# Which queue asks for the raw expert weights, and how a planner dates its loads, in a one-core decoder kernel

## The chip, the core and the metric

The kernel runs on one core of a Trainium2 chip. Its time is the device time of one execution in microseconds (us), the median of several runs. The engines are named as the profile names them: PE multiplies matrices, DVE works on vectors, ACT evaluates functions, POOL is a second, slower vector engine, and SP only issues transfers. POOL issues transfers too. Each engine works through its own instructions in order.

## What is computed

One decoder block in float32 on x of shape (16, 256, 256), with a layer norm after each of its three parts:

```python
x = _layernorm(x + attn(x))          # linear attention by cumulative sums, 32 heads
x = _layernorm(x + xattn(x, ctx))    # autocorrelation attention over the context
x = _layernorm(x + ffn(x))           # 8 experts in two branches, all of them weighted by a router
```

In the first part, a projection z = x @ in_proj_w is convolved over time. Its score columns give weights p = exp(...), its value columns give sines and cosines, and cumulative sums of these products over time are normalized, gated and projected back. The second part correlates queries and keys by Fourier transforms, keeps the best lags, and mixes the rolled values. In the third part, chains of weight matrices (W_Q with V_fwd, W_Q with W_inv and W_inv_exp, and so on) can be multiplied ahead of the data.

## The kernel before

**Stages.** The 16 sequences are worked on as 8 pairs. Each pair p goes through front (projection, convolution, scores; line 602), body (sines, cosines, cumulative sums, gating; 669), context (Fourier transform of the context and its keys and values; 896), back (924), attention (1056), router (1076) and experts (1152). Apart from the pairs, fold_weights (816) multiplies the weight chains once: it loads 18 tiles called raw (function raw, line 819; 256 KB each, but for one of 128 KB), multiplies them on PE into banks called w_ps, and ACT copies the products to the constants w_v, w_h, w_c and u_o, which router and experts read.

**Tile names.** In front, xc holds the transposed x, sc_ps and sc the scores (weights w_sc), in_ps and zc the projection (weights in_proj_w) and its convolution, ph the spread scores and g their product with a polynomial. In body, sn and ge are zc and g spread over partitions by transfers that SP issues (spread, line 665): zc must be ready, then sn is sent, then ACT takes sines of it, then DVE multiplies and sums. In context, ct is loaded, transformed through dft_ps, and multiplied in kv_ps. pv (line 516) holds small columns that front needs, and w_ri (521) is a small weight of body.

**Memory.** The raw tiles, the xc and ct tiles, and most tiles of context, router and experts share 19 slots of one size (SLABS, line 49; slab, line 493). A table of shares (line 461) lets raw tiles hold at most 11 of them at a time.

**The order.** No instruction is issued where it is written. Each call of an engine is noted (note, line 187), and at the end a planner (Work, line 114) decides the order and issues them all (give, line 445). Forward (273) simulates the engines with a cost for each instruction and always starts, on each engine, the ready instruction of lowest rank. The first rank is the place of the instruction's stage in the table PLACES (line 39). Backward (424) then gives each instruction a latest time from what comes after it: its readers, and the next instruction of its own engine. The latest times are the ranks of the next of 3 passes, and the shortest plan is kept.

**Loads.** A transfer that reads only inputs is marked as a fetch (line 208). From the second pass on, a fetch is not started before its latest time less 40 us (AHEAD, lines 122 and 276):

```python
ready = {o: max(0.0, late[o] - self.AHEAD) if late and o.fetch else 0.0 for o in self.ops}
```

Line 430 dates a fetch like every other instruction, so its latest time is also bounded by whatever follows it in the order of its issuing engine:

```python
t = min(end - o.lat, free[o.eng] - o.dur + self.LEAD[o.eng])
late[o], free[o.eng] = t, t
```

SP issues xc, in_proj_w, ct and all the transfers from tile to tile in front, body and experts. POOL issues every other load: pv, w_sc, the small constants, Wq, out_proj_w, the raw tiles, x, and the results.

Of the kernel before, what the change touches and what calls it, by code (L numbers as in the profile page):

```python
# [21 lines left out]
P = 128  # L22
# [14 lines left out]


PLACES = {
    "front": (0.95, 1.25, 4.3, 4.1, 4.0, 6.3, 4.8, 6.35, 8.75),  # L40
    "body": (0.35, -1.65, 1.6, 3.25, 1.95, 5.25, 3.85, 7.05, 8.6),
    "ctx": (0.85, 2.48, 1.4, 1.55, 1.9, 4.7, 0.3, 2.05, 2.55),
    "back": (3.4, -8.35, -6.05, -8.95, -7.9, -4.75, -7.45, -5.0, 0.8),
    "att": (0.1, -2.35, -3.95, -2.7, -6.8, 1.0, -0.0, 0.7, 3.5),
    "router": (0.35, 0.35, -2.05, 3.45, 4.3, 6.0, 5.65, 6.85, 5.55),
    "expert": (1.18, 3.85, 3.95, 5.85, 5.8, 8.6, 5.95, 9.15, 13.2),
    "fold": (6.5, 1.66),
}
EARLY, SLABS, XT_BUFS, ZC_BUFS, KBUFS, VBUFS, X_BUFS = 3, 19, 1, 4, 2, 3, 9
AHEAD = range(1, NP)  # L50
# [63 lines left out]
class Work:  # L114
# [72 lines left out]
    def note(self, eng, op, issue, args, kw):  # L187
        aps = [v for v in list(args) + list(kw.values()) if isinstance(v, bass.AP)]
        out = kw.get("out", aps[0])
        ins = [v for v in aps if v is not out]  # L190
        o = self.last
        if not (eng == "PE" and o and o.eng == "PE" and (self.joins or o.tiles[-1] == out.tensor.name)):
            o = Op(len(self.ops), eng, self.rank)
            self.ops.append(o)
        self.last = o
        o.parts.append((issue, args, kw))
        d, lat, o.lock = self.cost(eng, op, out, ins)
        if eng == "PE":
            r, c = ins[0].ap[0][1], self.columns(ins[0])
            r0, c0 = ins[0].offset // math.prod(ins[0].tensor.shape[1:]), out.offset // math.prod(out.tensor.shape[1:])  # L200
            cells = [(i, j) for i in range(r0 // 32, (r0 + r + 31) // 32) for j in range(c0 // 32, (c0 + c + 31) // 32)]
            o.mm.append((d, cells))
            o.shape = r, c
        else:
            o.dur, o.lat = d, lat
        if op == "dma_start":
            o.size = 4 * self.columns(out) * out.ap[0][1]
            o.fetch = not any(hasattr(i.tensor, "tag") for i in ins)
        if op == "activation":
            o.table = self.SETS.get(args[2])  # L210
        for ap in ins + [out]:
            t = ap.tensor
            if not hasattr(t, "tag"):
                continue
            write = ap is out
            p0, p1, f0, f1 = self.box(ap)
            self.tiles.setdefault(t.name, (t, []))[1].append(o)
            keep = []
            for a in self.users.get(t.name, ()):
                q, w, a0, a1, b0, b1 = a  # L220
                meets = q is not o and a0 < p1 and p0 < a1 and b0 < f1 and f0 < b1
                if meets and (w or write):
                    o.pre[q] = o.pre.get(q, False) or w
                if not (write and meets and p0 <= a0 and a1 <= p1 and f0 <= b0 and b1 <= f1):
                    keep.append(a)
            keep.append((o, write, p0, p1, f0, f1))
            self.users[t.name] = keep

            if t.name in o.tiles:
                o.tiles.remove(t.name)  # L230
            o.tiles.append(t.name)
# [192 lines left out]
    def backward(self, starts, span):  # L424

        free = dict.fromkeys(self.LEAD, span)
        late = {}
        for o in sorted(self.ops, key=lambda o: (-starts[o][1], -o.k)):
            end = min([span] + [late.get(q, span) - self.gap(o, q, q.pre[o]) for q in o.then])
            t = min(end - o.lat, free[o.eng] - o.dur + self.LEAD[o.eng])  # L430
            late[o], free[o.eng] = t, t
        return late

    def run(self, passes):
# [21 lines left out]
def decoder_kernel(ctx: ExitStack, tc: tile.TileContext, a: dict, out: bass.AP):  # L456
# [5 lines left out]
    V, S, G, T, Y = (  # L462
        Later(work, name, eng)
        for name, eng in (
            ("DVE", nc.vector), ("ACT", nc.scalar), ("POOL", nc.gpsimd), ("PE", nc.tensor), ("SP", nc.sync)
        )
    )
# [10 lines left out]
    def chunked(name):  # L478
        v = a[name]
        if len(v.shape) == 3:  # L480
            return v.rearrange("(c p) g n -> p c g n", p=P)
        return v.rearrange("(c p) n -> p c n", p=P)

    def load(name, shape, chunks=False, pool=const, eng=Y, tag=None):
        t = pool.tile(shape, F32, name=name, tag=tag or name)
        eng.dma_start(out=t, in_=chunked(name) if chunks else a[name])
        return t
# [5 lines left out]
    def slab(shape, name):  # L493
        return new(ff, shape, "slab", SLABS, name)
# [4 lines left out]
    def f_bank(name):  # L499
        return new(f_ps, [P, 512], "fps", 4, name)  # L500
# [13 lines left out]
    ident = const.tile([P, P], F32, name="ident", tag="ident")  # L514
    make_identity(nc, ident)
    pv = load("pv", [P, NPV], eng=G)
    w_in = load("in_proj_w", [P, 2, 2 * D], True)
    w_sc = load("w_sc", [P, 2, 2, 32], True, eng=G)
    tcol = load("theta_col", [P, 8], eng=G)
    ones_bd = load("ones_bd", [P, 8, 32], eng=G)  # L520
    w_ri = load("w_ri", [P, 2, K], eng=G)
# [294 lines left out]
    def fold_weights():  # L816
        work.rank = work.place("fold", 0, 0.0)

        def raw(name, n):

            if n <= D:
                t = slab([P, 2, n], "raw")
                G.dma_start(out=t, in_=chunked(name))
                return t[:, 0, :], t[:, 1, :]
            both = [slab([P, n], "raw") for _ in range(2)]
            for c in range(2):
                G.dma_start(out=both[c], in_=chunked(name)[:, c, :])
            return both

        def eights(ap, br):  # L830
            return ap.rearrange("p (n s e) -> p n s e", s=2, e=8)[:, :, br, :]

        def product(left, right, n, dst):

            for blk in range(2):
                ps = f_bank("w_ps")
                for c in range(2):
                    T.matmul(
                        ps[:, :n], left[c][:, blk * P : (blk + 1) * P], right[c], start=c == 0, stop=c == 1
                    )  # L840
                to = dst(blk)
                S.copy(to, ps[:, :n] if len(to.shape) == 2 else ps.rearrange("p (n e) -> p n e", e=8))

        wq_ = raw("W_Q", D)
        product(wq_, raw("V_fwd", KR), KR, lambda blk: eights(w_v[:, blk, :], 0))
        r1 = raw("r1t", D)
        product(wq_, r1, D, lambda blk: w_h[:, blk, 0, :])
        wk_ = raw("W_K", D)
        product(wk_, raw("W_fwd", KR), KR, lambda blk: eights(w_c[:, blk, :], 0))

        w_inv = raw("w_inv_t", D)

        def inverse_of(weight):
            t = slab([P, 2, D], "inv")
            product(w_inv, weight, D, lambda blk: t[:, blk, :])
            return t[:, 0, :], t[:, 1, :]

        iq = inverse_of(wq_)
        product(iq, raw("W_inv_exp", KR), KR, lambda blk: eights(w_v[:, blk, :], 1))
        product(iq, r1, D, lambda blk: w_h[:, blk, 1, :])  # L860
        product(inverse_of(wk_), raw("V_inv", KR), KR, lambda blk: eights(w_c[:, blk, :], 1))
        wo_, bt = raw("wot", D), raw("bt", P)
        for i, name in enumerate(("U_0", "U_1")):
            u = raw(name, KR)
            for half in range(2):
                lo = half * 2 * P
                product(
                    [t[:, lo : lo + 2 * P] for t in u], wo_, D, lambda blk: u_o[:, i * 4 + half * 2 + blk, :]
                )
        ps = f_bank("w_ps")  # L870
        for c in range(2):
            T.matmul(ps[:, :D], bt[c], wo_[c], start=c == 0, stop=c == 1)
        V.tensor_copy(b_o, ps[:, :D])
# [477 lines left out]
```

## Time and profile before

| | |
|---|---|
| median of 3 runs | 856.03 us (855.74 to 857.06) |
| the profiled execution | 857.1 us, its span in the profile 855.3 us |
| mean granted PE clock | 0.989 of full speed |
| busy PE / DVE / ACT / POOL | 812.4 / 700.0 / 581.8 / 256.9 us |
| chain of waits, largest shares | PE 65%, DVE 13%, ACT 8%, DMA 7% |
| transfers | 103.30 MB, mean 121 GB/s |
| first and last w_ps matmul | 24.4 and 72.1 us |

The slices cut the span into 40 equal parts, with one digit each: busy share in tenths. In the timeline a line gives the start in us, the duration in us, the engine, the line of the code, the instruction, what it writes and reads, and the count; the bracket at the end holds the idle time before it and what ended that. SPq is SP's queue of transfers. A line of the chain of waits gives start, duration and who held the path. Nearly all instructions carry line 452, since the planner issues them all there, so tiles are told apart by name.

### The profile page before, as it was taken

Reading aid. Unit: us, or ns where it says so; the run is one execution under the profiler, and the core shown is the slowest. Engines: PE = TensorE matmul, PEld = TensorE weight load, DVE = VectorE, ACT = ScalarE, POOL = GpSimd, SP = SyncE. Lnnn points to the kernel's source line nnn. Section 1 sums busy time; section 2 is a strip of 40 time slices with the busy share of each in tenths; the row PEclk is TensorE's granted clock in tenths of the full one; section 3 lists DMA queues with packets and bytes.
Section 4 is the critical chain, followed back from the end, with each engine's and each line's share of the span. In section 5 each row is a group of like instructions: output and inputs, shape, how many; then the busy total and the mean of one; then the engine's idle time right before and its main releaser. Section 6 shows DMA issues by size and latency. Waiting matters only on the chain.

```text
span 855.3 us, 12062 instructions
## 1 busy us (share of the span) xinstructions
PE 812.4 (95%) x4180; PEld 459.1 (54%) x4180; DVE 700.0 (82%) x1200; ACT 581.8 (68%) x862; POOL 256.9 (30%) x301
## 2 busy tenths in 40 slices
PE   4899989989999999999999999999999999999994
PEld 1355554455345564566445745565457457548453
DVE  5799599989998989998999999998979784472431
ACT  3899749777996798675987698678967632712601
POOL 7541356546122051243301501634004111221000
PEclk9899999999999999999999999999999999999997
DMA  8974675574376346633654456426463601130040
GB/s 270 328 177 107 192 196 170 145 200 124 75 173 144 74 102 145 161 85 59 168 124 110 92 116 150 124 50 163 107 138 66 150 22 47 53 72 1 25 99 25
DMA packets 58572, 103.30 MB, mean 121 GB/s; under 512 B 7744, under 2 KB 24160, under 8 KB 58512
## 3 DMA queue, kind: packets, MB, share of 16 engines
q1 hardware_dynamic: 48912, 71.85, 36.3%
q0 software_dynamic: 9600, 30.69, 11.3%
q8 instruction: 33, 0.54, 0.3%
q14 instruction: 27, 0.22, 0.1%
HBM read 28.06 MB, written 11.53 MB: 46 GB/s over the span
## 4 chain that ended last, share of the span: by engine, by line
PE 65%; DVE 13%; ACT 8%; DMA 7%; issue 4%; POOL 1%; SPq 1%; POOLq 0%; DVEq 0%; ACTq 0%
PE u_ps L452 13%; PE v_ps L452 10%; PE c_ps L452 9%; PE h_ps L452 6%; PE kv_ps L452 4%; DVE cs L452 3%; PE in_ps L452 3%; PE ss L452 3%; PE y L452 3%; ACT cs L452 2%; DVE sn L452 2%; PE q_ps L452 2%; PE out_ps L452 2%; DMA sn<-zc 2%; PE dft_ps L452 2%
## 5 line engine op out<-in xcount | busy, mean ns | idle before, releaser
L452 PE MATMUL c_ps<-fcT,w_c 128*128 128x512 f32 x256 | 120.2, 602 | 1.7 <-DVE dx L452 0.8
L452 PE MATMUL v_ps<-fxT,w_v 128*128 128x512 f32 x256 | 119.3, 600 | 1.7 <-ACT e L452 1.4
L452 PE MATMUL u_ps<-u_o,e 128*128 128x256 f32 x512 | 116.6, 382 | 0.3 <-DVE pp L452 0.3
L450 ACT ACT_TABLE_LOAD x89 | 114.2, 1283 | 1.6
L452 PEld LDWEIGHTS u_ps<-u_o,e 128*128 128x128 f32 x512 | 95.6, 190 | 19.9 <-issue 7.4
L452 DVE TENSOR_TENSOR_SCAN cs<-again,cs 128x1024 f32<-128x1024 bf16 x32 | 77.8, 2432 | 0.0
L452 PEld LDWEIGHTS c_ps<-fcT,w_c 128*128 128x128 f32 x256 | 46.5, 190 | 55.6 <-issue 46.6
L452 DVE SCALAR_TENSOR_TENSOR zc<-in_ps,pv,zc 128x510 f32<-128x510 f32 (+2 forms) x96 | 70.1, 736 | 6.3 <-ACT zc L452 5.6
L452 PEld LDWEIGHTS v_ps<-fxT,w_v 128*128 128x128 f32 x256 | 46.7, 190 | 53.0 <-issue 43.9
L452 DVE TENSOR_TENSOR_SCAN sn<-again,sn 128x1024 f32<-128x1024 bf16 x32 | 74.2, 2320 | 0.2
L452 PE MATMUL in_ps<-xc,in_proj_w 128*128 128x512 f32 x128 | 65.0, 636 | 5.1 <-DVE zc L452 4.9
L452 PE MATMUL kv_ps<-Wkv,specc 128*128 128x512 f32 x128 | 60.6, 608 | 0.9 <-DVE ks L452 0.4
L452 POOL TENSOR_TENSOR pp<-qf,kf 128x512 f32<-128x512 f32 (+1 forms) x32 | 45.1, 1429 | 52.4 <-ACT qf L452 37.3
L452 PE MATMUL h_ps<-fxT,w_h 128*128 128x512 f32 x128 | 59.4, 604 | 0.0
L452 DVE TENSOR_TENSOR e<-e,v_ps 128x512 f32<-128x512 f32 x64 | 43.0, 674 | 17.5 <-PE v_ps L452 17.3
L452 POOL TENSOR_TENSOR t<-vf,wf 128x256 f32<-128x256 f32 x32 | 22.6, 726 | 107.9 <-ACT wf L452 80.9
L452 POOL DMA_DIRECT2D out<-x x16 | 11.7, 731 | 131.9 <-ACT x L452 131.7
L452 POOL TENSOR_TENSOR g<-g,zc 128x512 f32<-128x512 f32 x16 | 24.0, 1497 | 83.0 <-ACT g L452 82.0
L452 ACT ACTIVATE sn<-sn,theta_col 128x512 f32<-128x512 f32 x64 | 44.7, 718 | 5.3 <-DMA sn<-zc 5.3
L452 DVE SCALAR_TENSOR_TENSOR cs<-cs,sn 128x1024 f32<-128x1024 f32 x32 | 40.3, 1259 | 9.2 <-ACT cs L452 9.2
L452 DVE TENSOR_TENSOR sn<-sn,ge 128x1024 f32<-128x1024 f32 x32 | 42.9, 1342 | 5.6 <-DMA ge<-g 3.8
L452 DVE TENSOR_TENSOR cs<-cs,ge 128x1024 f32<-128x1024 f32 x32 | 45.3, 1417 | 0.0
(220 smaller groups left out, 1589.4 us busy)
## 6 DMA issues: line engine op xcount, KB each, us to landing
sn<-zc SPq DMA_DIRECT2D x64, 256.0 KB
ge<-g SPq DMA_DIRECT2D x64, 256.0 KB
wb<-fwT SPq DMA_DIRECT2D x64, 256.0 KB
xc<-in_xT SPq DMA_DIRECT2D x16, 256.0 KB
ct<-in_ctx SPq DMA_DIRECT2D x16, 256.0 KB
x<-in_x POOLq DMA_DIRECT2D x16, 256.0 KB, 4.2
ph<-sc SPq DMA_DIRECT2D x64, 64.0 KB
gate<-zc SPq DMA_DIRECT2D x64, 64.0 KB
```

Source lines behind the costliest of these rows:

```text
L450: self.scalar.preload_act_table_set(self.TABLES[table])
L452: call(*args, **kw)
```

## The change

It has four parts. The raw tiles are loaded by SP (Y) and no longer by POOL (G). They no longer count as fetches, so that they may start from time zero. A fetch gets its latest time from its readers alone, and no longer bounds what its engine does ahead of it. And w_sc is loaded by SP, noted ahead of in_proj_w. PLACES has new values for most stages.

```diff
 PLACES = {
-    "front": (0.95, 1.25, 4.3, 4.1, 4.0, 6.3, 4.8, 6.35, 8.75),
-    "body": (0.35, -1.65, 1.6, 3.25, 1.95, 5.25, 3.85, 7.05, 8.6),
-    "ctx": (0.85, 2.48, 1.4, 1.55, 1.9, 4.7, 0.3, 2.05, 2.55),
-    "back": (3.4, -8.35, -6.05, -8.95, -7.9, -4.75, -7.45, -5.0, 0.8),
-    "att": (0.1, -2.35, -3.95, -2.7, -6.8, 1.0, -0.0, 0.7, 3.5),
-    "router": (0.35, 0.35, -2.05, 3.45, 4.3, 6.0, 5.65, 6.85, 5.55),
-    "expert": (1.18, 3.85, 3.95, 5.85, 5.8, 8.6, 5.95, 9.15, 13.2),
-    "fold": (6.5, 1.66),
+    "front": (0.95, 1.25, 4.3, 4.1, 3.6, 6.5, 4.85, 6.35, 8.75),
+    "body": (0.35, -1.85, 1.4, 2.85, 1.55, 4.85, 3.85, 6.65, 8.2),
+    "ctx": (0.85, 2.53, 1.5, 1.6, 1.95, 4.75, 0.35, 2.1, 2.6),
+    "back": (3.45, -7.85, -5.55, -8.35, -7.0, -3.95, -6.65, -4.3, 1.6),
+    "att": (0.8, -2.35, -3.95, -2.7, -6.8, 1.0, -0.0, 0.7, 3.5),
+    "router": (0.35, 0.75, -1.65, 3.85, 4.7, 6.4, 6.05, 7.25, 5.95),
+    "expert": (1.18, 3.05, 3.95, 5.85, 5.6, 8.6, 5.95, 9.35, 13.2),
+    "fold": (6.9, 1.66),
 }
...
-            o.fetch = not any(hasattr(i.tensor, "tag") for i in ins)
+            o.fetch = getattr(out.tensor, "source_name", None) != "raw" and not any(hasattr(i.tensor, "tag") for i in ins)
...
-            t = min(end - o.lat, free[o.eng] - o.dur + self.LEAD[o.eng])
-            late[o], free[o.eng] = t, t
+
+            t = end - o.lat if o.fetch else min(end - o.lat, free[o.eng] - o.dur + self.LEAD[o.eng])
+            late[o] = t
+            if not o.fetch:
+                free[o.eng] = t
...
+    w_sc = load("w_sc", [P, 2, 2, 32], True)
     w_in = load("in_proj_w", [P, 2, 2 * D], True)
-    w_sc = load("w_sc", [P, 2, 2, 32], True, eng=G)
...
                 t = slab([P, 2, n], "raw")
-                G.dma_start(out=t, in_=chunked(name))
+                Y.dma_start(out=t, in_=chunked(name))
...
             for c in range(2):
-                G.dma_start(out=both[c], in_=chunked(name)[:, c, :])
+                Y.dma_start(out=both[c], in_=chunked(name)[:, c, :])
```

## The prediction

> **What bounds the kernel now.** I read the page's slices first, for three rows: two engines and the transfers.
>
> ```profile
> PE   4899989989999999999999999999999999999994
> DVE  5799599989998989998999999998979784472431
> DMA  8974675574376346633654456426463601130040
> ```
>
> One digit is 21.4 us. PE is full everywhere but in the first two slices and the last one. DVE is nearly full up to slice 32. The transfers are heaviest in the first two slices, just where PE is not busy. So I asked for the busy time by stage (columns: length; PE, PEld, DVE, ACT, POOL busy with instruction counts; granted clock; DMA share; GB/s):
>
> ```profile
> 0.00:42.00 42.00, 26.57 (x92) 10.92 (x93) 27.21 (x65) 23.42 (x33) 27.85 (x49) 0.92 0.94 301
> 42.00:100.00 58.00, 56.56 (x321) 33.29 (x320) 49.49 (x55) 51.94 (x82) 19.76 (x21) 1.00 0.59 149
> 100.00:700.00 600.00, 585.34 (x3164) 328.19 (x3163) 558.00 (x918) 457.17 (x663) 188.84 (x205) 1.00 0.52 125
> 844.00:855.30 11.30, 0.05 (x2) 0.00 (x0) 3.29 (x12) 2.37 (x5) 1.45 (x2) 0.61 0.13 46
> ```
>
> PE is idle 42.9 us of 855.3: 15.4 before 42 us, 11.3 in the tail after its last matmul, 16.2 in all the rest. Between 100 and 700 us PE is 98% busy and DVE 93%: both bound it together. What is loose is the start. There PE's own timeline reads:
>
> ```profile
> 8.11 1.93 PE L452 MATMUL sc_ps<-xc,w_sc 128*32 128x256 f32 x16 [8.11 <-DMA w_sc<-in_w_sc]
> 9.97 5.53 PE L452 MATMUL in_ps<-xc,in_proj_w 128*128 128x512 f32 x8
> 19.14 5.45 PE L452 MATMUL in_ps<-xc,in_proj_w 128*128 128x512 f32 x8 [3.64 <-DVE zc L452]
> 24.42 5.32 PE L452 MATMUL w_ps<-raw 128*128 128x512 f32 x16
> 33.62 3.28 PE L452 MATMUL w_ps<-raw 128*128 128x512 f32 x4 [2.17 <-ACT w_v L452]
> ```
>
> PE waits 8.1 us for w_sc, and in the 3.64 us hole it has nothing but fold products to do, whose raw weights are not there. The timeline of POOL and SP shows why, and the chain of waits shows what DVE waits for:
>
> ```profile
> 5.07 0.71 POOL L452 DMA_DIRECT2D Wq<-in_Wq  x1
> 7.25 0.54 POOL L452 DMA_DIRECT2D c_mean<-in_c_mean  x1 [0.91 <-DMA pv<-in_pv]
> 16.48 0.71 POOL L452 DMA_DIRECT2D raw<-in_W_Q  x1
> 41.95 0.57 POOL L452 DMA_DIRECT2D raw<-in_U  x1 [6.14 <-PE w_ps L452]
> ```
> ```profile
> 3.16 1.50 SPq L452 DMA_DIRECT2D xc<-in_xT  x2
> 15.28 3.94 SPq L452 DMA_DIRECT2D ph<-sc  x6
> ```
> ```profile
> 4.01 6.64 DMA w_ri<-in_w_ri
> 21.28 9.42 DMA sn<-zc
> ```
>
> The first raw weight is asked for at 16.48 us, behind loads such as Wq, whose first reader starts at 111.0 us. SP issues nothing from 4.66 to 15.28 us. DVE's path goes through the landing of w_ri (6.64 us) and of the first spreads (9.42 us).
>
> **The change, part by part.**
>
> *Raw loads leave POOL.* 18 issues at 0.54 to 0.76 us, 11.0 us by their rows, and four waits for slots in front of U loads, 13.1 us together (longest 6.14). POOL's next computation waits for ACT anyway (g at 19.99 us for 0.28, at 56.09 for 5.02), so the freed time is worth nothing by itself; I count 0. Loads queued behind them on POOL (f_dft, Wkv, bo) come up to some us sooner, and nobody waited for these.
>
> *Raw loads go to SP, at once.* An unhindered SP issue takes 0.43 us (xc: two in 0.87). The slab share allows 11 of the 18 before any slot is freed: 11 x 0.43 = 4.7 us, with w_sc 5.2 us, inside the 10.6 us hole. The other seven (3.0 us) lie among the spreads. The ninth DMA of a queue waits for the landing of its first (c_mean, ninth on POOL, for pv), so SP also stands still until earlier loads land. By 330 GB/s (the rate of 4 to 16 us), pair 0's xc, in_proj_w and w_sc (1.1 MB) and 11 raw tiles (2.9 MB) are in 12 us after they begin, about at 14 us, before ph at 15.28. Cover: this hole. If the flood is not over when sc is ready, ph and then sn queue behind it one for one.
>
> *Other loads by their readers alone.* They may be asked for 40 us ahead of their readers (the planner's constant). Wq (read at 111), out_proj_w (92.65), c_corr, f_roll, c_roll, the first ct (dft at 72.28) and the first x need not run before 16 us: 0.26 + 0.52 + 0.39 + 0.20 + 0.13 + 0.52 + 0.52 = 2.5 MB, or 7.7 us of transfers. The raw tiles' 2.9 MB take that place. 40 us is far more than the slowest landing (9.8 us, Wkv), so being late costs 0.
>
> *A rule against it.* The Trainium skill (DMA: Bandwidth & Descriptors, "Issuing engines are not separate DMA queues") says that SP and POOL feed the same 16 DMA engines and that another issuer saves only issue time. The DMA share of 0.94 over 42 us fits. By the rule alone only unused transfer time is to be won: 0 to 4 us (share 0.52) and 16 to 18 (0.70) leave 1.9 + 0.6 = 2.5 us, or 853.5 us. But the rule speaks of bandwidth, not of which bytes come first: the row of Wq at 5.07, 106 us ahead of its use, says that the order is wrong. So I go by the rows.
>
> *What PE gets.* Before 42 us it idles 15.4 us. It also runs slow: 16 sc_ps take 1.93 us where later ones take 1.04; the two groups of 8 in_ps take 5.53 and 5.45 us where the chain has 1.72 for four; the w_ps of 33.62 take 3.28 for four such. That is 0.9 + 2.1 + 2.0 + 1.5 = 6.5 us. The Trainium skill (TensorE: Matmul & The Clock Gate, "What's actually happening") puts such half pace down to an idle window of about 3.4 us; the granted clock shows it in 20 to 24 us (0.63, 0.52), yet it reads 1.00 at 10 to 12 while the matmuls take 0.69 us each. By the granted clock alone the loss there would be nothing, by the durations 2.1; I take the durations. So 21.9 us of PE time lie open. What remains lost: about 6 us until xc and w_sc land (pv, issued at 1.49, landed at 6.99), 2.5 us of slow matmuls, 2 or 3 us of holes. Fold is 29 us of PE at full pace (32 matmuls at 0.43, 68 at 0.22, as the groups of 12 and 20 run), and enough of its weights land between 8 and 14 us. Its evictions (24 copies, 10.5 us on ACT) now meet an ACT that is busy 7 of the 20 us from 4 to 24. PE's lead at 42 us: 21.9 - 11 = about 11 us.
>
> *What DVE gets.* w_ri is issued one POOL slot (0.72 us) earlier: 0.7. The first sn: 8 raw loads (2.1 MB, 6.4 us of transfers) were issued beside it and would now be in. Bounds: 0 if the late seven and the ring ahead take their place, 9.42 - 3.65 = 5.8 if it lands as a later ge on the chain does (3.65 us). Nearer to the latter, since most of the competitors go: 4.0. Lead: 4.7 us.
>
> *The new order.* All places change by up to 0.8 and the planner orders all 800 us anew. No row shows that. From 100 to 200 us PE idles 7.1, from 200 to 300 2.8: one plan's stretches differ by 4.3 us, so I bound it by -4.3 and +4.3 and take 0; neither sign has a reason.
>
> *The sum.* Up to 700 us PE can run ahead of DVE only as far as it has work that DVE does not feed. Fold was such filler until 74 us; once it is done early, only the context stage (kv_ps, dft_ps) replaces it. So DVE's 4.7 us count in full and of PE's further 6.3 I take a quarter, 1.6: together 6.3 us. From the profiled execution's 857.1 us (span 855.3 and 1.8 around it): 850.8. That execution lies 1.1 above the median, so against 856.03: **849.7 us**.
>
> **Rivals.**
> - *Lead given back.* PE finishes fold early and then waits for pair 0 between 42 and 100 us; DVE gets only the 0.7 of w_ri. For: pv's landing at 6.99 us and the sp chain after it do not move, and DVE's front work hangs on both. Against: the 9.42 us landing is plainly crowded. 855.3 us.
> - *SP stands in front of the spreads (slower).* The seven loads beyond the share wait on SP for PE to free a slot, as POOL did for 13.1 us. Behind them in SP's order stand sn, ge, ph and gate of pairs 0 and 1, for which ACT and then DVE wait. On POOL such a wait cost nobody anything; on SP it delays spreads one for one. It decides from the point where a slot comes free later than the next spread's source. One wait of the longest kind, 6.1, before a spread cancels the 6.3 gained; two waits cost 11 to 12 of the 13.1: 856 - 6.3 + 11.5 = 861 us. Against: fold runs earlier, so slots come free earlier.
> - *The full lead.* Context filler suffices and all 11 us of PE arrive, with the order 2 us better: 843 us.
>
> That the change doesn't do what it says is hardly possible: the issuing engine is written in the code.
>
> **How the numbers follow.** Likeliest case 0.50 (845.4 to 854.0, which is 849.7 less and more 4.3), full lead 0.12, lead given back 0.13, SP in the way 0.25. About 0.2% (1.7 us) is what a measurement of this kernel can tell from no change. Faster 0.62, same 0.13, slower 0.25. Range 842 to 862: it takes in the full lead and the centre of the slower case.
>
> **What would show it.** Right: w_sc and W_Q on SP before 5 us, first matmul near 6, w_ps before 12 us and its last before 60 (before: 72.1); Wq asked for after 50 us; the landing of the first sn on the chain below 7 us; PE idle before 42 us below 10. Given back: PE idle from 42 to 100 us grows from 1.4 to over 6. SP in the way: SP's waits on PE w_ps in front of sn or ge grow from 1.0 us, and ACT sn waits for DMA for more than the 2.1 us of the first 45. I am wrong altogether if PE's 14.7 us of idle time between 100 and 700 us change by more than 5: then the new order decides, not the loads.

## The result, and the profile after

The change takes 871.15 us (median; 870.33 to 873.04) against 856.54 (855.74 to 857.9) beside it: ratio 1.0168, interval 1.0139 to 1.0198. It is slower, and outside the forecast range. The profiled execution took 870.45 us with a span of 868.2. (In the quoted expectations TensorE, VectorE, ScalarE, GpSimd and SyncE are PE, DVE, ACT, POOL and SP.)

The same three rows of the page, with digits of 21.7 us each:

```profile
PE   7898998969979998999999998999999999999995
DVE  5388879999999999997989999998899854463341
DMA  8837678464665354715647336533645511040040
```

PE's first digits rose from 4 and 8 to 7 and 8, as forecast. DVE's second and third fell from 7 and 9 to 3 and 8, and PE has two low digits, 6 and 7 in slices 9 and 12, where it had 8 and 9. The busy time by stage gives the sizes:

```profile
0.00:42.00 42.00, 32.97 (x114) 17.69 (x115) 20.08 (x58) 24.64 (x40) 10.64 (x21) 0.96 0.87 255
42.00:100.00 58.00, 55.51 (x310) 29.95 (x309) 50.27 (x51) 42.66 (x73) 32.28 (x31) 1.00 0.55 149
100.00:700.00 600.00, 565.92 (x3133) 320.64 (x3132) 555.30 (x926) 464.51 (x669) 188.91 (x206) 0.99 0.53 128
```

PE's idle time is 9.0 us before 42 us (it was 15.4), 2.5 up to 100 us (1.4) and 34.1 from 100 to 700 us (14.7). So 6.4 us were won at the start and 20.5 lost after it; with -0.2 in the rest that is 13.9 of PE's time, and the span grew by 12.9. The loss is spread: 7.0, 3.5, 1.3, 2.0, 5.8 and -0.2 us in the six stretches of 100 us. PE's waits from 100 to 700 us (total, times, longest) do not name one place either:

```profile
PE kv_ps L455 <- ACT specc L455: 5.8, 3, 3.5
PE y L455 <- DVE cs L455: 5.7, 4, 3.2
PE out_ps L455 <- DVE gate L455: 4.9, 2, 4.5
```

The start shows what the new plan does. PE's timeline:

```profile
6.46 1.93 PE L455 MATMUL sc_ps<-xc,w_sc 128*32 128x256 f32 x16 [6.46 <-DMA xc<-in_xT]
8.33 3.67 PE L455 MATMUL in_ps<-xc,in_proj_w 128*128 128x512 f32 x4
11.83 7.04 PE L455 MATMUL w_ps<-raw 128*128 128x512 f32 x20
...
34.77 1.88 PE L455 MATMUL in_ps<-xc,in_proj_w 128*128 128x512 f32 x4
...
43.37 1.88 PE L455 MATMUL in_ps<-xc,in_proj_w 128*128 128x512 f32 x4
...
59.15 1.88 PE L455 MATMUL in_ps<-xc,in_proj_w 128*128 128x512 f32 x4
```

The raw weights are there at 12 us, as wanted. But the folding of weights now runs ahead of the first pair's own projections: three of their four groups come at 34.8, 43.4 and 59.2 us, where all four were done by 25 us before. The table PLACES puts the fold at 1.66 in both kernels and those groups at 1.77, 1.92 and 2.06: by that first rank the fold stands ahead of them in both kernels, and what held it back before was that its weights came late (the first was asked for at 16.48 us). SP and DVE of the changed kernel:

```profile
25.07 4.66 SPq L455 DMA_DIRECT2D ph<-sc  x3
29.91 0.58 SPq L455 DMA_DIRECT2D ge<-g  x1
30.60 1.88 SPq L455 DMA_DIRECT2D raw<-in_U  x2
```
```profile
28.83 1.23 DVE L455 SCALAR_TENSOR_TENSOR cs<-cs,sn 128x1024 f32<-128x1024 f32 x1 [7.14 <-ACT cs L455]
37.33 1.23 DVE L455 TENSOR_TENSOR sn<-sn,ge 128x1024 f32<-128x1024 f32 x1 [4.29 <-DMA ge<-g]
```

DVE's first cs is 3.7 us earlier than before (32.52). Then it waits 4.29 us for ge: g was done at 20.7 us, but SP sends ge only at 29.9, behind raw weights and ph.

### The profile page after: what moved, and what is told of

Its sections match the earlier page's. It is cut to its first block, busy times and chain, and to the rows that moved or that the text cites. A ratio compares the mean times of both kernels' runs of the same rounds, so it can differ in the third digit from the quotient of the medians.

```text
span 868.2 us, 12060 instructions
## 1 busy us (share of the span) xinstructions
PE 811.4 (93%) x4180; PEld 461.5 (53%) x4180; DVE 696.8 (80%) x1200; ACT 580.2 (67%) x862; POOL 250.8 (29%) x282
## 4 chain that ended last, share of the span: by engine, by line
PE 48%; DVE 14%; ACT 12%; issue 5%; DMA 2%; SPq 0%; POOLq 0%; POOL 0%; DVEq 0%; ACTq 0%
PE u_ps L455 11%; PE v_ps L455 9%; PE c_ps L455 8%; PE h_ps L455 5%; DVE cs L455 5%; ACT cs L455 3%; ACT L453 3%; PE wo_ps L455 2%; DVE sn L455 2%; ACT sn L455 2%; PE out_ps L455 2%; PE q_ps L455 2%; PE in_ps L455 2%; DVE e L455 2%; DMA wb<-fwT 2%
## 5 line engine op out<-in xcount | busy, mean ns | idle before, releaser
L455 DVE SCALAR_TENSOR_TENSOR zc<-in_ps,pv,zc 128x506 f32<-128x506 f32 (+2 forms) x96 | 69.3, 734 | 5.0 <-ACT zc L455 4.7
L455 POOL TENSOR_TENSOR dx<-dx,bo 128x256 f32<-128x256 f32 x16 | 22.3, 1396 | 145.3 <-PE dft_ps L455 145.3
L455 PE MATMUL in_ps<-xc,in_proj_w 128*128 128x512 f32 x128 | 62.6, 615 | 0.0
L455 ACT ACTIVATE ge<-sn 128x1024 f32<-128x1024 f32 x32 | 33.8, 1057 | 26.2 <-DVE sn L455 21.6
L455 POOL TENSOR_TENSOR bothc<-ct 128x256 f32<-128x256 f32 x32 | 38.4, 1222 | 38.8 <-PE w_ps L455 19.1
L455 DVE TENSOR_TENSOR sn<-sn,ge 128x1024 f32<-128x1024 f32 x32 | 40.8, 1275 | 9.6 <-DMA ge<-g 5.6
L455 POOL TENSOR_TENSOR t<-vf,wf 128x256 f32<-128x256 f32 x32 | 20.0, 644 | 93.3 <-ACT wf L455 75.1
```

Of the source, the lines that this page charges most:

```text
L455: call(*args, **kw)
```

## Experiments

**The theory** after this profile: the order that the planner made for all 800 us is worse, whatever the loads do. **Rivals:** raw weights on SP stand in front of the spreads; or the start alone (fold ahead of the first pair, ge late) is carried to the end. A further one came up on the way, POOL's count of transfers. "Old order" means that the planner's order of before is kept and only transfers are moved in it. Ratios are to the kernel before, timed beside each run. The diffs are shortened to what they do.

### Old order, raw weights on SP

```diff
+        move(raws[:11], load("in_proj_w")[0])   # SP, directly behind in_proj_w
+        move(w_sc, xc[1])
-        call(*args, **kw)
+        (sync.dma_start if target in ("raw", "w_sc") else call)(*args, **kw)
```

> The kernel before with its planned order kept: PE, DVE, ACT and all transfers but these keep their places; SP, not POOL, issues w_sc and the 18 raw loads, w_sc after xc and the first 11 raw tiles right after in_proj_w. Theory 'the new order costs the time': the transfers themselves do no harm and save up to what the first spreads gain, 850 to 857 us. Rival 'SP stands in front of the spreads': 861 us or more, with the landing of the first sn and ge later than before. Rival 'transfers crowd the start': PE's first matmul or pv later than before by over 2 us, 858 to 862 us.

862.11 us, ratio 1.007 (1.0037 to 1.0104).

```profile
21.34 4.04 SPq L470 DMA_DIRECT2D ph<-sc  x6
```
```profile
36.62 1.23 DVE L470 SCALAR_TENSOR_TENSOR cs<-cs,sn 128x1024 f32<-128x1024 f32 x1 [5.00 <-ACT cs L470]
```

ph goes out at 21.34 us instead of 15.28, and the first cs begins 4.1 us later than before (32.52). SP stands in front of the spreads, as the rival has it, though not by the raw weights alone: behind them SP also sent two ct and two xc, until 19.8 us, and where these stand behind the spreads, ph goes at 13.81 us with the same 11 raw weights ahead of it ("other loads deferred" below). The second rival, a crowded start, falls: PE's first matmul comes at 5.76 us (before 8.11). The 4.1 us at the first cs are not what the time at the end consists of either ("five transfers on the old order").

### The change, raw weights issued by POOL again

```diff
-                call(*args, **kw)
+                (pool.dma_start if o.eng == "SP" and target == "raw" else call)(*args, **kw)
```

> The kernel after with its planned order kept; only the issuing engine of the 18 raw loads is POOL again. Theory 'order': the order of PE, DVE and ACT is that of after, so the time stays within 3 us of 871 us. Rival 'SP in the way': SP's queue is rid of 18 loads, ge is sent several us sooner (after: 29.9 us, its g ready at 20.7), and 4 to 10 us come back: 861 to 867 us.

869.55 us, ratio 1.0154 (1.0119 to 1.0189).

```profile
26.16 4.34 SPq L466 DMA_DIRECT2D ge<-g  x4
```
```profile
26.40 1.23 DVE L466 SCALAR_TENSOR_TENSOR cs<-cs,sn 128x1024 f32<-128x1024 f32 x1 [5.05 <-ACT cs L466]
```

The start recovers: ge goes out 3.7 us sooner than in the change, the first cs begins 2.4 us sooner, and ACT's sn waits 1.7 us for transfers in the first 45 us instead of 5.8. Little of it arrives: of the 14.6 us the issuing engine owes 1.2 (by the ratios) to 1.6 us (by the medians). The intervals overlap, so it may be nothing, and they do not exclude some us more.

### The change, first pair ahead of the fold; then ge ahead as well

In the change's order, the three late groups of in_ps go in front of the fold's products with their ACT and DVE steps; the second kernel adds the lines on ge.

```diff
+        for m, pe, act, dve in first_pair[1:4]:
+            put(pe, ahead=w_ps[...]); put(act, ahead=...); put(dve, ahead=...)
...
+        ges = load("ge")[:4]
+        move(ges, g)      # on SP directly behind g, ahead of raw bt, U and ph
```

> The kernel after with its planned order kept but for one thing: pair 0's three later in_ps products, their first conversion on ACT and their nine convolution steps on DVE are put ahead of the fold products, into the hole that DVE has from 21.7 to 28.8 us. Theory 'fold has overtaken pair 0 and DVE starves': DVE's busy time before 42 us rises from 20 to about 27 us and most of these 6.7 us arrive at the end, 863 to 867 us. Rival 'the order of the whole run is worse': DVE is repaired at the start but the time stays at 869 to 871 us.

> The change with its first pair's projections put ahead of the folding of the weights, as in the earlier run (868.6 us), and SyncE's four ge spreads of that pair issued right behind g, ahead of the raw weights bt and U and of ph, so that ge goes out some 9 us earlier (it went at 29.9 us in the change, g being done at 20.7). Theory (the order of the whole run decides, the start is a few us): 865 to 869 us, PE idle between 100 and 700 us still 28 us or more. Rival (the start's queue on SyncE is most of the loss, and what it costs is carried to the end): 856 to 862 us.

868.61 us, ratio 1.0161 (1.0112 to 1.0211), and 868.33 us, ratio 1.014 (1.0103 to 1.0176). Stages of the first:

```profile
0.00:42.00 42.00, 34.49 (x123) 18.65 (x124) 27.67 (x68) 25.64 (x42) 12.73 (x23) 1.00 0.86 257
42.00:100.00 58.00, 55.61 (x309) 29.90 (x308) 45.35 (x43) 44.55 (x76) 30.41 (x34) 1.00 0.58 161
100.00:700.00 600.00, 568.08 (x3133) 322.49 (x3133) 555.23 (x925) 460.75 (x664) 185.65 (x203) 0.98 0.53 127
```

DVE's start is repaired (27.67 us busy before 42 us, against 20.08 in the change and 27.21 before), but PE still idles 31.9 us between 100 and 700 us. So the start as a whole is worth 0.6 to 2.8 us (ratios and medians of the two), hardly more than can be told from nothing, and the rest lies in the order behind it.

### One load changed, planned anew; and the change at the old PLACES

The first kernel is before with this edit alone, at the old PLACES; the second is the whole change with only PLACES set back.

```diff
+    w_sc = load("w_sc", [P, 2, 2, 32], True)
     w_in = load("in_proj_w", [P, 2, 2 * D], True)
-    w_sc = load("w_sc", [P, 2, 2, 32], True, eng=G)
```

> The kernel before with one part of the change: SP loads w_sc, noted ahead of in_proj_w; the planner plans anew at the old places. By itself this moves one 64 KB load and costs or saves at most 2 us: 854 to 858 us if only the load counts. Theory 'the places fit one plan alone, and any change of the loads throws the plan off': clearly slower, 870 us or more, with PE's idle time between 100 and 700 us grown from 14.7 us to 25 or more.

> The whole change but for the table PLACES, which is that of before; planned anew. Theory 'places belong to one set of loads': slower than before by 15 us or more (870 to 900 us), with PE's idle time between 100 and 700 us at 30 us or more. Rival 'the new places are the fault': 850 to 860 us.

909.11 us, ratio 1.0623 (1.0586 to 1.0661), and 885.3 us, ratio 1.035 (1.0328 to 1.0372). From 100 to 700 us, the first and the second:

```profile
100.00:700.00 600.00, 553.80 (x2962) 313.02 (x2961) 524.15 (x855) 429.30 (x629) 193.12 (x202) 0.97 0.49 122
```
```profile
100.00:700.00 600.00, 556.02 (x2997) 316.86 (x2996) 541.01 (x878) 458.64 (x648) 186.77 (x197) 0.96 0.51 124
```

One 64 KB load put on another queue costs 52 us once the planner orders everything again: PE idles 46.2 us there. That size points to the new order and not to the one transfer, and so does the planner's own end of the plan, which moves from 825.8 to 882.7 us.

### The change with PLACES searched anew

Only the numbers of PLACES differ from the change; two independent searches. Both put the fold behind some of the first pair's four groups: 2.26 behind three of them, 2.1 behind two.

```diff
-    "fold": (6.9, 1.66),
+    "fold": (6.29, 2.26),
...
```

> The whole change, with only the numbers of PLACES searched anew for its own loads (the planner's own end of the plan: 834.4 us, against 850.6 for the change as it is and 825.8 for before). Theory (the order decides: places fit one set of loads, and the change's were not good ones): the run takes 853 to 862 us, at least 9 us less than the change as it is, and PE's idle time between 100 and 700 us falls from 34.1 to below 24 us. Rival (the loads themselves cost: raw weights in SyncE's queue in front of the spreads, and loads that come late to their readers): 866 to 872 us, with PE idle between 100 and 700 us above 28 us.

> The whole change with a second, independently found set of PLACES (the planner's own end: 835.5 us). Theory (the order decides): 854 to 864 us; the two sets differ by no more than about 4 us. Rival (the loads cost, whatever the order): 866 to 872 us.

860.06 us, ratio 1.0043 (1.0021 to 1.0066), and 859.55 us, ratio 1.0023 (1.0006 to 1.0041).

```profile
100.00:700.00 600.00, 577.08 (x3111) 323.27 (x3110) 550.15 (x909) 462.13 (x660) 204.84 (x205) 0.99 0.52 127
```
```profile
100.00:700.00 600.00, 573.72 (x3125) 322.82 (x3122) 548.51 (x918) 473.33 (x672) 190.67 (x205) 0.99 0.53 126
```

The same loads and the same issuing engines: 11 to 12 us come back. In the first, PE idles 22.9 us between 100 and 700 us, within the forecast; in the second 26.3. The theory holds for the larger part of the loss. No run has a new set for the loads of before, so what a search would have gained there is not shown. The planner's own end of the plan puts the rows in the order in which the chip has them:

| loads | PLACES | plan ends, us | measured, us |
|---|---|---|---|
| before | before | 825.8 | 856.5 |
| change | new, first / second search | 834.4 / 835.5 | 860.1 / 859.6 |
| change | change | 850.6 | 871.2 |
| change | before | 859.2 | 885.3 |
| w_sc alone | before | 882.7 | 909.1 |

### Old order, other loads deferred

To the first run of this section: ct, bothc, the second pair's xc, Wq, c_corr and five more loads, and two x, are issued later, so that the raw weights have the transfers to themselves. In the second kernel the fold's products move up by four as well.

```diff
+        move(ct[:2] + bothc, ge[3])
+        move([Wq, c_corr, c_mean, f_roll, c_roll, out_proj_w, w2t, x, x], bo)    # POOL, 36 to 47 us
```

> As e1 (planned order of before; SP issues w_sc and the raw tiles at the start), and in addition the loads that nobody reads soon are put off, as the change does: the first two ct behind pair 0's spreads, Wq, c_corr, c_mean, f_roll, c_roll, out_proj_w, w2t and two x behind bo on POOL; pair 1's xc right behind the first four sn. Theory 'e1 lost its 4.7 us because ct and xc stood behind the raw tiles and ahead of ph on SP (ph at 21.3 us, its data ready at 13.5)': ph is sent by 16 us, the first cs step of DVE comes at or before 32.5 us (before) and the time is 851 to 857 us. Rival 'the raw loads' own volume delays the spreads': first cs after 34 us and 859 us or more.

> As e5, and the fold products are moved up by four: two stand between pair 0's in_ps products, two behind them, and all later ones take the place of the one four before; the rest of the order is that of before. Theory of the prediction, with the order left alone: PE's hole before 24 us is filled with some 5 us of work and 1 to 5 us of it arrive, 848 to 854 us. Rival 'DVE alone sets the pace after the start': PE's idle time only moves to after 42 us and the time is that of e5 within 1 us.

863.44 us, ratio 1.0081 (1.0063 to 1.01), and 867.03 us, ratio 1.0137 (1.0105 to 1.017): both far above what their theories gave. SP and DVE in the first:

```profile
13.81 3.94 SPq L480 DMA_DIRECT2D ph<-sc  x6
```
```profile
28.70 1.23 DVE L480 SCALAR_TENSOR_TENSOR cs<-cs,sn 128x1024 f32<-128x1024 f32 x1 [1.56 <-ACT cs L480]
...
56.27 1.23 DVE L480 SCALAR_TENSOR_TENSOR cs<-cs,sn 128x1024 f32<-128x1024 f32 x1 [3.26 <-ACT cs L480]
```

The first cs is 3.8 us earlier than before: at that place the DVE lead of the prediction is real. The third cs is 1.6 us later than before (54.72): the deferred loads now collide with the spreads that it needs (DMA share 1.03 and 1.04 from 42 to 50 and 50 to 56 us, against 0.79 and 0.92). In the second kernel moved-up products meet raw weights that are not sent yet:

```profile
PE w_ps L495 <- DMA raw<-in_U: 10.2, 2, 8.6
```

### Old order, late loads in the transfers' hole

```diff
-        move(late + x[:2], bo)          # POOL, 36 to 47 us
+        move(late + x[:3], bothc[5])    # POOL, about 66 us
```

> Order of before, raw weights and w_sc on SyncE at once, as in the run with deferred loads, but Wq, c_corr, c_mean, f_roll, c_roll, out_proj_w, w2t and three tiles of x are issued by GpSimd behind the six bothc products of the start (about 66 us), where the transfers of before are idle (DMA share 0.03 to 0.06 between 60 and 70 us), instead of at 36 to 47 us. The first of them to be read is out_proj_w, at 94 us. Theory (the early raw weights are worth a lead of VectorE of about 4 us, and the deferred loads then took it back by standing in front of the second pair's spreads): DMA share of 42 to 56 us falls from 1.03 to 0.9 or less, PE busy between 42 and 100 us returns from 51.9 to 55 or more, and the run takes 852 to 856 us (ratio to before 0.995 to 1.000). Rival (the lead has no taker: the written order makes the second pair as late as before whatever the loads do): 857 to 861 us. Rival (fixed cost of raw weights in front of the spreads on SyncE's queue): 860 to 863 us.

857.82 us, ratio 1.0019 (1.0 to 1.0038): not the 852 to 856 of the theory, but in the range of its first rival (the lead has no taker). DVE's lead over before, read from the starts of the same instruction (cs<-cs,sn):

```
start in before, us        32.5   88.2  129.9  260.8  440.2  569.5  595.3  679.1
late loads in the hole     -3.4   -0.7   -4.9   -4.2   -3.4   -3.3   +1.0   +1.2
old order, first run       +4.1   +4.1   +1.0   +2.2   +4.5   +5.2   +9.5   +9.7
```

(Negative is earlier. The traced execution of the old order took 866.8 us, 4.7 above its median, so its row shows more than the usual loss.) Of the first lead of 3.4 us 0.7 is left at 88 us, as that rival has it. Another 4.2 us come between 88 and 130 us; the old order wins 3.1 there too, so they do not come from the first spreads ("five transfers on the old order" shows from what). And both kernels lose 4.3 us between 570 and 595 us. POOL there, in this kernel and in the kernel before:

```profile
579.47 1.20 POOL L482 TENSOR_TENSOR t<-vf,wf 128x256 f32<-128x256 f32 x2
583.06 0.59 POOL L482 DMA_DIRECT2D vf<-vf_away  x1 [2.39 <-DMA sn<-zc]
583.65 1.65 POOL L482 COPY lg<-lg 128x512 f32<-128x512 f32 x1
```
```profile
582.80 1.20 POOL L452 TENSOR_TENSOR t<-vf,wf 128x256 f32<-128x256 f32 x2
584.29 0.58 POOL L452 DMA_DIRECT2D vf<-vf_away  x1 [0.30 <-POOL t L452]
584.96 0.60 POOL L452 COPY lg<-lg 128x512 f32<-128x512 f32 x1
```

vf starts 2.39 us behind the two t that it names, where 0.30 us stood before; sn is only the profile's guess at the releaser. The copy behind it takes 1.65 us instead of 0.60, PE waits 2.75 us for that copy, and the four matmuls of in_ps behind that pause take 3.18 us instead of 1.88. Old order with and without deferred loads show the same 2.39 us at this vf.

### What the stall at vf depends on

In all kernels of this order so far with the raw weights and w_sc on SP, that vf is POOL's transfer number 93; before, it was number 112. Three kernels add something on POOL ahead of its first g, in idle time: 20 one-element memsets, five transfers of 4 KB, or 18 of them.

```diff
+        for n in range(5):                            # before the first g on POOL
+            pool.dma_start(out=pad[:, n], in_=theta_col)
```

> The run with the late loads in the transfers' hole (857.8 us), with 20 one-element memsets added on GpSimd ahead of its first g, in idle time of that engine. They do no work; they put every later GpSimd instruction at about the number in its stream that it had in the kernel before (the raw weights' 18 issues are gone from that stream). In that run VectorE was 3.3 us ahead of before at 566 us, and lost 4.3 us between 580 and 590 us, where GpSimd's issue of vf began 2.4 us after all that it names had been done; VectorE and TensorE then waited. In three runs with the order of before and the raw weights on SyncE the same 2.39 us stood at the same instruction, at 583, 589 and 592 us. Counted from the program, with one more for each further wait of an instruction, that issue is number 261 of GpSimd's stream there and 282 in the kernel before; the Trainium skill (Runtime: NRT & Kernel Launch, Instruction fetch mechanics) states that instructions are fetched in blocks of 256. Theory (the stall belongs to the place in GpSimd's stream, a block of instructions that comes late): the 2.4 us at that vf go away, VectorE is 2 us or more ahead of before at 660 us, and the run takes 851.5 to 855 us. Rival (the stall belongs to what vf waits for, SyncE's sn or the order): it stays at that vf, and the run takes 856.5 to 859 us.

> The run with the late loads in the transfers' hole (857.8 us), with five 4 KB transfers added on GpSimd ahead of its first g, into a tile that nothing reads. vf at 583 us then is GpSimd's 98th transfer, and the 93rd is an out at about 533 us, behind which GpSimd has nothing urgent for 7 us. Theory (GpSimd stands still for some 2 us at about its 93rd transfer, whatever that is): the 2.39 us at vf go away, a stall of 1 to 3 us may show at an out or x between 530 and 545 us, VectorE is 2 us or more ahead of before at 660 us, and the run takes 852 to 855.5 us. Rival (the stall belongs to the place in the order): it stays at vf, 856.5 to 859 us.

> The same with eighteen such transfers, as many as the raw weights and w_sc were: vf is then number 111, as in the kernel before, and the 93rd falls between 370 and 400 us. They take some 10 us of GpSimd's time between 7 and 19 us and may delay its first g (17 us) and the first pair by 0 to 3 us. Theory (number of transfers): no stall at vf, VectorE 0 to 4 us ahead of before at 660 us, 852 to 857 us. Rival (place in the order): the stall stays at vf, 857 to 861 us.

Memsets: 858.19 us, ratio 1.0003 (0.9976 to 1.0029), with the 2.39 us still at vf (581.11 us). The theory of a late block of 256 instructions falls. Five transfers: **852.33 us, ratio 0.9957 (0.994 to 0.9973)**, faster than before and than the change. Eighteen: 854.7 us, ratio 0.998 (0.9958 to 1.0003). POOL with five transfers:

```profile
577.56 1.19 POOL L486 TENSOR_TENSOR t<-vf,wf 128x256 f32<-128x256 f32 x2
579.05 0.58 POOL L486 DMA_DIRECT2D vf<-vf_away  x1 [0.30 <-POOL t L486]
579.71 0.61 POOL L486 COPY lg<-lg 128x512 f32<-128x512 f32 x1
```

The stall at vf is gone, the copy takes 0.61 us again, and the lead stays: 5.25 us at 569.5 and at 679 us, and 3.36 at both with eighteen. That is the 4.3 us which the kernel without them loses there; the other 2 us of lead at 569.5 us, and so the rest of the 5.5 us at the end, lie elsewhere (with the memsets it was 5.27 too).

The same transfer in several kernels of this order shows where the stall went. An x with five transfers and without, an out with eighteen (0.00 us in the other kernels), and a kf in before (0.00 in the others):

```profile
540.39 0.76 POOL L486 DMA_DIRECT2D x<-in_x  x1 [2.41 <-DVE dx L486]
```
```profile
540.18 0.75 POOL L482 DMA_DIRECT2D x<-in_x  x1 [0.30 <-DVE almv L482]
```
```profile
406.00 0.73 POOL L486 DMA_DIRECT2D out<-x  x1 [2.11 <-ACT sn L486]
```
```profile
376.94 0.60 POOL L452 DMA_DIRECT2D kf<-kf_away  x1 [1.68 <-issue]
```

The three that stand still are POOL's transfers number 94, 98 and 94, and the vf is number 93. So before had the stall as well, where nobody waited for it, and it goes by what POOL has transferred and not by the place in the order; but not by the count alone. Count one for each transfer and a sixteenth of the pieces that its record in the trace names (128 for kf and vf, 256 for x and out): the sum goes from 1,022 to 1,031 at the kf, from 1,021 to 1,030 at the vf, from 1,014 to 1,031 at the x and from 1,010 to 1,027 at the out, so all four pass about 1,025. This is a fit to the traces, which no run tested, and its cause is not shown; with both new sets of PLACES no idle time stands at that transfer.

### The five transfers on the old order and on the change

> The order of before with the raw weights and w_sc on SyncE at once (862.1 us, ratio 1.007), plus five 4 KB transfers on GpSimd ahead of its first g. In that run VectorE was 4.1 us behind before at 92 us, 5.2 at 570 and 9.5 at 595, behind the 2.39 us stall at vf. Theory (two separate costs, the spreads behind the raw weights on SyncE and the stall at GpSimd's 93rd transfer): the stall at vf goes, 4.1 us of lateness at 92 us stay, and the run takes 856.5 to 860 us. Rival (the five transfers only helped by moving something else, the bo load for one): 861 to 863 us.

> The whole change (871.15 us) plus the same five transfers. There the 93rd transfer of GpSimd is an x at 592.5 us that nothing reads soon, and TensorE was busy 9.7 to 10 of each 10 us around it. Theory (the order is the change's cost, the stall is hidden): 869 to 872 us. Rival (GpSimd's transfer count costs the change as well): 864 to 868 us.

859.31 us, ratio 1.0023 (1.0008 to 1.0038), and 872.22 us, ratio 1.0168 (1.0139 to 1.0196). On the old order the stall at vf is gone and with it more than half of the 5 us (862.11 to 859.31; the two intervals touch). DVE is 5.0 us late up to 93 us there, behind what SP sent first, but only 0.8 us at 130 us and 0.5 at 679. It catches up at two DVE instructions that are long in before, each beside a bothc of POOL:

```profile
108.97 3.35 DVE L452 TENSOR_TENSOR cs<-cs,ge 128x1024 f32<-128x1024 f32 x1
109.12 1.42 POOL L452 TENSOR_TENSOR bothc<-ct 128x256 f32<-128x256 f32 x2
...
123.90 3.81 DVE L452 TENSOR_TENSOR_SCAN cs<-again,cs 128x1024 f32<-128x1024 bf16 x1
124.12 1.43 POOL L452 TENSOR_TENSOR bothc<-ct 128x256 f32<-128x256 f32 x2
```

With five transfers the same two take 1.22 and 2.26 us, 3.7 us less, and the first of these pairs of bothc comes later and takes 4.34 us itself, beside two scans of DVE. That DVE and POOL hold each other up there is read from these rows and was not tested. The 3 to 4 us that the kernels above win against before at this place then come from how DVE and POOL meet there, in kernels that arrive later than before as in those that arrive earlier, and not from earlier loads. The change itself gains nothing from the five transfers: its stall, 1.70 us at an x at 592.5 us that nothing reads soon, moves to an out at 586.4 us.

## Why the prediction was wrong, point by point

- **"The new order ... I bound it by -4.3 and +4.3 and take 0"** is the step that failed. With the change's loads held fixed, four sets of PLACES gave 859.6, 860.1, 871.2 and 885.3 us. Against a set found for these loads, the change's own costs 11 to 12 us. I sized the step by how uneven one good plan is inside, which says nothing about how much worse another plan can be. There was a reason for a sign as well: PLACES and loads belong together, and a change of loads throws the plan off (52 us for w_sc alone). The prediction's last sentence named the sign, PE's idle time from 100 to 700 us changing by more than 5: it changed by 19.4.
- **PE's lead.** First matmul at 6.46, w_ps at 11.83 and ended by 49.6, Wq asked for at 112.6 us: as foreseen. PE's idle time before 42 us is below 10 as foreseen. The lead is 6.4 us by idle time alone; in the prediction's own terms, with the matmuls done by 42 us counted at its full paces, it is 8.2 (20.4 us of work before, 28.5 after), not 11. And it was bought with DVE's time: the products overtook the first pair, and DVE had 20.1 us done at 42 us where it had 27.2.
- **DVE's lead of 4.7 us** is there at the first cs: 3.7 us in the change, and 1.9 to 3.9 us in six traces of the old order with the other loads out of its way. That it "counts in full" is not borne out. In the four of them with the late loads in the hole, 0.7 to 2.9 us of it are left at 88 us, and what later cs show beyond that goes with the two long instructions of before. (In the change the first sn is there 3.8 us after it is sent, at 21.60 us for 17.77, within the 7 foreseen.) With five transfers the whole gain at the end is 3.7 us (852.33 against 856.03) of the 6.3 summed; how much of it is this lead is not shown.
- **Late loads cost 0.** In the old order not at 36 to 47 us: with those loads there 863.4 us, in the hole 857.8. My reason, that 40 us exceeds the slowest landing, looked only at their readers and not at the spreads beside them.
- **Raw loads leave POOL, counted at 0.** In the change that held (872.2 against 871.2 us), though SP's first 11 issues took 8.3 us (2.73 to 11.03) and not the 4.7 summed. In the order of before it put the stall onto vf: without it the medians are 2.8 us (862.1 to 859.3) and 5.5 us (857.8 to 852.3) lower, and the traces show 4.3 us at that place.
- **SP in front of the spreads** exists: 4.1 to 5.0 us at 93 us in the old order, and ge 9 us late in the change. Both of its signs came: in the change SP's waits on PE w_ps grew to 3.8 us, and ACT's sn waited 5.8 us for transfers in the first 45 us. But the price at the end is 2 us in the old order (859.3 against 857.1 beside it) and 1.2 to 1.6 in the change (POOL as issuer), not 11.5. That this rival gave the right sign of the result was luck: it was not the cause.
- **The rule against the change** (another issuer saves only issue time) is borne out by these small prices. What it leaves out is who stands behind the transfer in the issuer's order: ph at 21.34 us or at 13.81 with the same raw weights ahead.

Of the 14.6 us, 11 to 12 come back with new PLACES. The start (0.6 to 2.8) and the issuer (1.2 to 1.6) were undone with the change's order held; they may be parts of those 11 to 12 or stand beside them. The 2 to 3.7 us that stay with the new sets were not traced to one cause.

## What to carry to other kernels

If a planner with tuned places makes the order, a change of one load is a change of every instruction's position: tune the places again before judging the loads, and compare the plans' own ends, or keep the old order and move only the transfers. Ask of a stage that comes late what holds it back, its rank or its data: data that come early may let it overtake the critical one. And when a lead appears in the trace but not in the time, follow one repeated instruction through both traces and look at every place where the difference jumps, those in the kernel before included.

## What the runs showed of the hardware that was not expected

In most of these traces one of POOL's transfers stands still for some 2 us, and which one it is depends on the number and size of those before it. Five transfers of 4 KB, which nothing reads, made a kernel 5.5 us faster, 4.3 of them where a stall of 2.39 us no longer fell on a transfer that PE was soon to wait for; 20 memsets did not. And PE was slow behind its pause of 2.75 us: four matmuls of 128x512 took 3.18 us there, against 1.88, with a granted clock of 0.83 in that stretch (580 to 590 us) against 1.00 before.

```profile
585.35 1.08 PE L482 MATMUL wt_ps<-ident,lg 128*128 128x128 f32 x4 [2.75 <-POOL lg L482]
586.23 3.18 PE L482 MATMUL in_ps<-xc,in_proj_w 128*128 128x512 f32 x4
```
